# The first attention stage's score row: two transfers over DRAM in place of two TensorE transposes

## The chip, the cores and the metric

The kernel runs on one core of a Trainium2 chip. The metric is the device time of one execution in microseconds (us), as the median of several runs. A profile is one execution taken by the hardware profiler; its time is a little longer than that of a run without it. The engines are PE (TensorE matmul, with PEld for its weight loads), DVE (VectorE), ACT (ScalarE), POOL (GpSimd) and SP (SyncE, which here only issues DMAs).

## The reference: what is computed

64 graphs of 256 nodes with 256 features go through two layers. The first layer is two graph-attention stages, a layer norm, a feed-forward block and a layer norm; the second is attention over 8 heads with relations, and a feed-forward block. Only the first graph-attention stage matters here:

```python
def _gat(h, adj, W, a, out_features):
    Wh = jnp.matmul(h, W)
    Wh1 = jnp.matmul(Wh, a[:out_features])
    Wh2 = jnp.matmul(Wh, a[out_features:])
    e = Wh1 + jnp.swapaxes(Wh2, 1, 2)
    e = jax.nn.leaky_relu(e, negative_slope=ALPHA)
    scores = jnp.where(adj > 0, e, NEG)
    att = jax.nn.softmax(scores, axis=1)
    return jnp.matmul(att, Wh)
```

A score is the sum of one number of the one node (Wh1) and one number of the other (Wh2). With one of the nodes on the partitions, the numbers of those nodes are a column, one per partition, and the numbers of the others are a row of 256, which every partition needs in full. The change is about how that row gets to all partitions.

## The kernel before

All 64 graphs ("batches") are worked on at staggered stages. The work of a batch is cut into pieces with short names; the order in which all engines get them is written out by hand in three lists. PERIOD is one turn of the steady state: `F.fb/3` means that the piece F.fb is issued for the batch three behind the newest. It runs 58 times (batches enter it one by one, and the pieces of one turn belong to seven batches). START and END list the pieces of the first and the last batches with their batch numbers (`G.wh0:1` is batch 1, `T.out:-1` the last). Within an engine the instructions run in exactly this order; between engines, semaphores order them. All DMAs of the steady state go through SP's one queue, also in this order: an issue that waits for an engine holds up all later issues.

The pieces near the change, with their lines:

- G.wh0, G.wh1 (`project`, L847): PE multiplies the transposed input by the joint weights, which gives Wh and four columns of scores. G.wc0, G.wc1 (`keep`, L864): ACT copies the two halves to the SBUF tile wh_A. In PERIOD, wc0 of a batch is near the end of one turn and wc1 in the next.
- G.eA (`targets`, L870): two PE transposes of a score column of wh_A, each broadcast over 128 columns first, so that the row of 256 arrives in every partition of a PSUM tile e.
- G.lrA (`terms`, L884): ACT adds the other column as a bias and applies ReLU, from e in PSUM to s in SBUF, one instruction for each half of the nodes. G.adA (`maximum`, L893 to L899): DVE adds the row's linear part, masks, and takes the maximum. G.exA (`exps`, L910): ACT takes exponentials, from e to s. G.gA0, G.gA1 (`first`, L930): PE multiplies by Wh.
- G.eB to G.gB are the same for the second graph-attention stage; G.gB (`second`, L930, tile gat_b) is PE's last use of the buffer s in a batch. s has one buffer for both stages and all batches.
- The `turned` helper (L542, L546, L553) turns a tile by 32 x 32 squares on DVE (dt), writes it to DRAM (dm, tiles far_...) and reads it back as columns in four transfers (mg). It serves the attention's probabilities p (far_p, then pm, keys 10, 11, 01, 00) and the layer norms' outputs (far_y_a and cols_a after the first norm, far_y_y and cols_y after the second, far_y_c and cols_c after the third).
- F.qa to F.qe (L967, tile qX, qY, qZ): PE's projections to queries and keys, which read cols_y. F.sB (L676, tile S_y): POOL's sums of blocks of cols_y for the same projections.

PSUM has 8 banks for all products, given out in turn (`mm_tile`). DMAs share 8 semaphores in turn, so an issue also waits for the landing of the eighth before it.

The turn's order around the change, as it was (a piece of PERIOD): `F.nmB/3 T.hk1/5 G.lnA/2 T.hb/5 F.dtB/3 T.hk2/5 G.rsA/2 T.hp1/5 A.sp01/4 A.dm01/4 T.hc/5 A.mg10/4 T.hk3/5 G.nmA/2 F.raB/4 F.dtA/2 T.hd/5 A.vk2/4 G.most/1 T.hp3/5 G.eA/1 T.hp2/5 T.ge0/5 F.dmB/3 F.dmA/2`.

Of the kernel before, what the change touches and what calls it, by code (L numbers as in the profile page):

```python
# [25 lines left out]
F32 = mybir.dt.float32  # L26
# [8 lines left out]
P = 128  # L35
# [14 lines left out]
F.nmB/3 T.hk1/5 G.lnA/2 T.hb/5 F.dtB/3 T.hk2/5 G.rsA/2 T.hp1/5 A.sp01/4 A.dm01/4 T.hc/5 A.mg10/4  # L50
T.hk3/5 G.nmA/2 F.raB/4 F.dtA/2 T.hd/5 A.vk2/4 G.most/1 T.hp3/5 G.eA/1 T.hp2/5 T.ge0/5 F.dmB/3
F.dmA/2 T.fp2/6 A.sp00/4 A.vc/4 A.vp1/4 T.rbC/5 A.vk3/4 T.he/5 A.pm13/4 F.mgB/3 A.vp3/4 A.pm10/4
F.sB/3 G.lrA/1 F.mgA/2 A.vd/4 A.pm11/4 T.ge1/5 G.wh0/0 T.hk4/5 T.fe/6 G.wc0/0 F.qa/3 T.ge2/5
F.qk1/3 A.vp2/4 A.dt00/4 F.qb/3 A.ve/4 F.qk2/3 G.adA/1 F.qc/3 F.qk3/3 F.qp1/3 F.sA/2 F.ha/2 F.qp3/3
T.ge3/5 G.exA/1 F.qd/3 F.qp2/3 T.fk4/6 A.vk4/4 T.u0/5 F.hb/2 F.qe/3 A.mg01/4 F.hk1/2 A.sc1/3
T.lnD/6 F.hp1/2 A.mx11/3 F.hk2/2 A.dm00/4 A.pm03/4 A.mg00/4 T.u1/5 A.mx13/3 F.hc/2 A.mx10/3 F.hk3/2
A.ex13/3 A.mx12/3 T.rsD/6 L.adj/0 F.hp3/2 F.qk4/3 F.hd/2 A.pm02/4 F.hp2/2 A.ex12/3 A.pm01/4
# [10 lines left out]
G.wh0:0 G.wc0:0 G.wh1:0 G.wc1:0 G.eA:0 S.wf:0 S.f0:0 W.b:8 G.lrA:0 G.away:0 G.adA:0 G.exA:0 G.rzA:0  # L68
G.gA1:0 L.xT:2 G.most:0 L.adj:1 L.xT:1 S.f1:0 G.gA0:0 G.wd1:0 G.wd0:0 G.eB:0 G.wh0:1 G.lrB:0
G.adB:0 G.exB:0 W.b:3 S.wk:0 L.xT:3 G.rzB:0 G.wh1:1 W.c:8 S.wv:0 G.gB:0 G.lnA:0 S.f2:0 G.rsA:0  # L70
G.wc0:1 G.wc1:1 G.eA:1 S.v0:0 S.q0:0 G.lrA:1 S.p0:0 W.d:1 G.nmA:0 G.wh1:2 F.dtA:0 G.away:1 F.dmA:0
G.adA:1 G.exA:1 F.mgA:0 G.wh0:2 G.wh1:3 F.sA:0 G.rzA:1 F.ha:0 S.q1:0 F.hb:0 F.hk1:0 F.hk2:0 S.j1:0
S.lr:0 F.hc:0 F.hk3:0 F.hd:0 L.x:1 F.hp1:0 G.gA0:1 F.hp3:0 F.hp2:0 F.raA:0 F.rbA:0 F.r0:0 F.he:0
F.r1:0 G.gA1:1 F.hk4:0 F.r3:0 F.r2:0 G.most:1 F.u0:0 L.adj:2 G.wd1:1 F.u1:0 W.d:7 G.wd0:1 F.fa:0
F.fb:0 F.u3:0 G.eB:1 S.j2:0 F.fk1:0 S.lx:0 F.fk2:0 F.u2:0 F.fc:0 F.fk3:0 F.fd:0 G.lrB:1 G.adB:1
F.fp2:0 F.fp1:0 G.away:2 G.exB:1 F.fe:0 F.fp3:0 G.rzB:1 G.wc1:3 F.fk4:0 S.q2:0 F.lnB:0 G.wc1:2
F.rsB:0 G.gB:1 F.nmB:0 G.lnA:1 G.wc0:2 G.eA:2 F.dtB:0 G.rsA:1 G.nmA:1 G.most:2 F.raB:0 G.wh0:3
W.b:7 F.raA:1 F.dtA:1 F.dmB:0 F.mgB:0 F.dmA:1 G.lrA:2 W.a:3 W.b:4 G.adA:2 F.sB:0 F.qa:0 G.exA:2
F.qb:0 G.wc0:3 F.qk1:0 F.qk2:0 F.qc:0 F.rbA:1 F.qk3:0 G.rzA:2 F.qp3:0 F.mgA:1 F.qd:0 F.sA:1 F.qp2:0
A.sc1:0 L.xT:4 A.mx12:0 F.qe:0 A.mx10:0 L.adj:3 F.ha:1 G.away:3 A.ex12:0 F.hk1:1 F.qk4:0 A.mx11:0  # L80
F.hb:1 S.p2:0 F.hk2:1 F.hc:1 F.hk3:1 A.rz12:0 F.hp1:1 F.qp1:0 A.sp12:0 A.mx13:0 F.hd:1 A.ex10:0
F.hp2:1 A.sc0:0 L.x:3 A.ex13:0 A.rz13:0 A.sp13:0 A.ex11:0 F.hp3:1 A.mx00:0 A.rz11:0 F.he:1 F.r0:1
S.v1:0 G.gA1:2 F.hk4:1 A.mx03:0 S.lw:0 L.x:2 F.r1:1 A.rz10:0 A.sp11:0 G.gA0:2 A.mx02:0 S.v2:0
F.r3:1 F.r2:1 A.sp10:0 A.dt10:0 F.fa:1 G.wd1:2 F.u0:1 A.dt11:0 G.wd0:2 G.eB:2 A.dm10:0 G.lrB:2
F.fk1:1 F.fb:1 F.u1:1 A.mx01:0 F.fp1:1 F.fk2:1 F.u3:1 A.ex03:0 F.fc:1 F.fk3:1 A.ex02:0 F.u2:1
A.dm11:0 F.fd:1 G.adB:2 G.exB:2 F.fp2:1 L.x:4 F.fp3:1 A.rz03:0 A.mg10:0 S.v3:0 G.rzB:2 F.fe:1
G.most:3 F.fk4:1 F.lnB:1 F.rbB:0 A.mg11:0 F.rsB:1 A.rz02:0 G.gB:2 G.wh1:4 F.nmB:1 A.vb:0 A.va:0
A.sp02:0 G.lnA:2 F.dtB:1 A.vk2:0 A.ex00:0 G.rsA:2 G.nmA:2 A.ex01:0 A.vk1:0 S.l0:0 A.vc:0 F.dtA:2
F.dmB:1 F.raB:1 A.rz01:0 A.vp1:0 F.dmA:2 G.wh0:4 A.vk3:0 A.pm11:0 A.sp03:0 S.l1:0 A.rz00:0 F.mgB:1
G.eA:3 G.lrA:3 F.sB:1 A.vd:0 F.mgA:2 G.wc0:4 A.vp2:0 F.qa:1 A.sp01:0 A.sp00:0 F.qb:1 F.qk1:1  # L90
A.vp3:0 A.dt01:0 F.qk2:1 A.dm01:0 A.ve:0 G.wc1:4 F.qc:1 L.xT:5 F.sA:2 F.qp1:1 F.qk3:1 G.adA:3
F.ha:2 F.qd:1 F.hk1:2 A.vk4:0 F.qp3:1 A.dt00:0 A.mg01:0 G.exA:3 F.qp2:1 A.pm12:0 F.hb:2 F.hp1:2
A.sc1:1 F.hk2:2 G.rzA:3 F.hc:2 A.pm10:0 A.mx12:1 A.mx13:1 A.dm00:0 A.ex12:1 F.raA:2 A.pm13:0
A.mx11:1 A.o1:0 A.rz12:1 A.ex13:1 F.rbA:2 A.rz13:1 L.adj:4 F.hk3:2 A.mx10:1 G.gA0:3 F.hd:2 F.qe:1
A.ex10:1 A.mg00:0 A.sp13:1 G.wd0:3 A.ex11:1 A.sp12:1 F.hp3:2 G.gA1:3 A.rz10:1 F.qk4:1 G.wd1:3
A.pm02:0 F.hp2:2 A.sp10:1 A.rz11:1 A.pm03:0 A.sp11:1 F.r0:2 A.oc1:0 A.dt11:1 F.r1:2 F.he:2 A.pm00:0
A.dm11:1 F.hk4:2 F.r2:2 F.r3:2 A.pm01:0 G.eB:3 A.dt10:1 A.sc0:1 F.u0:2 A.mx03:1 G.lrB:3 A.o0:0
A.oc0:0 G.adB:3 A.dm10:1 A.ex03:1 F.u1:2 F.u3:2 F.fa:2 T.wo:0 F.fk1:2 F.u2:2 G.exB:3 F.fb:2 T.lnC:0
T.rsC:0 A.mg11:1 F.fk2:2 F.fc:2 S.l2:0 A.mx00:1 G.rzB:3 F.fk3:2 F.fd:2 F.fp1:2 T.nmC:0 A.vb:1
A.ex00:1 F.fp2:2 F.fe:2 A.mg10:1 T.dtC:0 F.fp3:2 A.mx02:1 G.gB:3 T.dmC:0 A.ex02:1 F.fk4:2 F.lnB:2  # L100
F.rsB:2 A.va:1 A.vk1:1 A.vk2:1 A.vc:1 F.nmB:2 T.mgC:0 A.rz03:1 G.wh0:5 A.mx01:1 G.eA:4 G.away:4
G.lnA:3 G.rsA:3 A.vk3:1 F.dtB:2 A.rz02:1 G.most:4 A.vd:1 A.rz00:1 G.wc0:5 F.dmB:2 G.nmA:3 A.sp03:1
T.sC:0 F.dtA:3 T.ha:0 G.lrA:4 T.hk1:0 A.vp2:1 T.hb:0 A.vp1:1 A.ex01:1 F.mgB:2 F.dmA:3 A.rz01:1
A.sp02:1 T.hk2:0 A.sp01:1 A.ve:1 T.hc:0 G.adA:4 A.dt01:1 A.sp00:1 A.vk4:1 T.hk3:0 F.sB:2 T.hd:0
T.hp2:0 F.qa:2 G.exA:4 T.raC:0 F.qk1:2 F.qb:2 F.qk2:2 F.qc:2 T.hp3:0 A.dt00:1 A.pm11:1 F.qk3:2
F.mgA:3 T.he:0 F.qd:2 T.ge0:0 F.sA:3 T.ge1:0 F.qp3:2 T.hp1:0 T.hk4:0 A.pm13:1 T.ge2:0 F.qp2:2
F.ha:3 A.dm01:1 T.ge3:0 F.qp1:2 F.hk1:3 A.vp3:1 F.hb:3 A.sc1:2 F.qe:2 F.hk2:3 F.rbB:1 A.mx10:2
F.qk4:2 A.dm00:1 T.rbC:0 F.hp1:3 A.mg01:1 A.mg00:1 A.mx12:2 A.pm12:1 A.mx11:2 F.hc:3 A.pm10:1
A.mx13:2 A.pm02:1 F.hk3:3 T.fa:0 A.pm03:1 T.u0:0 A.ex11:2 A.ex13:2 A.rz13:2 F.hd:3 A.ex12:2
A.ex10:2 G.rzA:4 A.pm00:1 F.hp2:3 T.fb:0 T.u1:0 A.sp13:2 A.pm01:1 T.fk1:0 A.rz11:2 A.o1:1 A.o0:1  # L110
A.rz10:2 F.raA:3 A.oc1:1 A.oc0:1 F.hp3:3 F.r1:3 L.adj:5 A.rz12:2 F.he:3 T.u3:0 F.hk4:3 F.r2:3
T.fp1:0 T.wo:1 A.sp12:2 T.fk2:0 A.dt11:2 T.lnC:1 T.fc:0 A.sp11:2 G.away:5 A.sp10:2 F.r3:3 A.dm11:2
T.fk3:0 T.fp3:0 T.rsC:1 F.rbA:3 G.gA1:4 F.r0:3 T.nmC:1 A.sc0:2 F.u0:3 A.mx02:2 F.fa:3 G.wd1:4
A.ex02:2 G.gA0:4 F.fk1:3 A.mx03:2 A.dt10:2 T.dtC:1 A.mg11:2 F.u1:3 A.rz02:2
# [4 lines left out]
T.u2:-6 F.fp1:-3 A.vk1:-4 T.dmC:-5 A.pm13:-4 G.rzB:-2 T.mgC:-5 F.fe:-3 A.ex01:-4 A.vb:-4 F.fk4:-3  # L119
T.sC:-5 G.gB:-2 F.lnB:-3 G.eA:-1 T.fd:-6 F.rsB:-3 A.sp02:-4 A.ex00:-4 A.vk2:-4 F.nmB:-3 A.vp1:-4  # L120
G.lnA:-2 A.vc:-4 G.lrA:-1 A.mg10:-4 T.fp2:-6 G.rsA:-2 T.ha:-5 F.dtB:-3 A.vk3:-4 A.rz03:-4 T.hk1:-5
A.rz00:-4 G.nmA:-2 A.rz01:-4 A.sp01:-4 L.x:-1 G.adA:-1 T.hp1:-5 T.hb:-5 A.sp03:-4 T.hk2:-5
# [88 lines left out]
def binary(ctx: ExitStack, tc: tile.TileContext, t, most, out: bass.AP):  # L211
# [612 lines left out]
    def gat(do, b, tiles):  # L824
# [40 lines left out]

        def targets(step, col):

            t["e"] = mm_tile(f"e_{step}{b}", (P, NT, N))
            for i in range(NT):
                nc.tensor.transpose(  # L870
                    parts(t["e"])[:, 0, 2 * i : 2 * i + 2],
                    t["wh", step][:, i, col : col + 1].to_broadcast([P, P]), ident,
                )
# [4 lines left out]
        def terms(step, col):  # L878
            if "early s" in tiles:
                s = t["s"] = tiles["early s"]  # L880
            else:
                s = t["s"] = work.tile([P, NT, N], F32, tag="s", name=f"s_{step}{b}", bufs=1)
            for j in range(NT):
                nc.scalar.activation(  # L884
                    parts(s)[:, j], parts(t["e"])[:, 0], AF.Relu,
                    bias=t["wh", step][:, j, col : col + 1],
                )

        def maximum(step):

            s, e = parts(t["s"]), parts(t["e"])
            for j in reversed(range(NT)):
                nc.vector.scalar_tensor_tensor(  # L893
                    e[:, j], e[:, 0], ALPHA / (1.0 - ALPHA), s[:, j], ALU.mult, ALU.add
                )
# [52 lines left out]
        for step, src, tgt, width in (("A", SRC1, TGT1, X2), ("B", SRC2, TGT2, D)):  # L948
            do[f"G.e{step}"] = partial(targets, step, tgt)
            do[f"G.lr{step}"] = partial(terms, step, src)  # L950
            do[f"G.ad{step}"], do[f"G.ex{step}"] = partial(maximum, step), partial(exps, step)
            do[f"G.rz{step}"] = partial(over_sums, step, width)
# [529 lines left out]
```

## Time and profile before

| | |
|---|---|
| median of 3 runs | 2992.03 us (2991.58 to 2992.23) |
| the profiled execution | 2993.21 us |
| span of its instructions | 2991.4 us |
| granted TensorE clock over the span | 0.995 |
| DMA queue of SP | 399,984 packets, 442.14 MB, 46.7% of 16 engines' time |
| matmul of e_A (L870) | x124 in the page's tile view and x4 in early batches, 273 ns each |
| ReLU of stage A (L884) | 457 ns each |

How to read the profile: the busy share of an engine counts the union of its instructions' times. Matmuls are pipelined and their ends are modelled, so what a matmul costs PE is read from the start of one to the start of the next. L12 is line 12 of the kernel before. In the timeline a row is: start in us from the span's start, duration in us, engine, line, operation, what it writes <- what it reads, and how many; in brackets, the idle time of the engine before it and what ended that. SP's rows are issues of DMAs: their duration is that of the issue, not of the transfer. In the chain of waits, a row is a start, a duration and what took it.

### The profile page before, as it was taken

To read this page: it belongs to the slowest core of one execution; us is meant where nothing else is said; L and a number is where in the kernel's file an instruction comes from. 1 tells how busy PE (TensorE), PEld (TensorE's weight loads), DVE (VectorE), ACT (ScalarE), POOL (GpSimd) and SP (SyncE) were. 2 spreads that over 40 slices of the span, in tenths; PEclk is the share of its full clock that TensorE was granted. 3 is DMA by queue.
4 is the path that set the end of the run, shared out by engine and by line. 5 is a ranking of instruction groups with operands and counts; after the bars stand their busy time and mean duration, and the time that the engine had idled before them with its cause. 6 is when DMAs were issued, how large, how long until landed. Compare 5 with 4: busy or idle time off the path is not lost.

```text
span 2991.4 us, 75422 instructions
## 1 busy us (share of the span) xinstructions
PE 2947.1 (99%) x25662; PEld 2672.7 (89%) x25662; DVE 2599.5 (87%) x6247; ACT 2232.7 (75%) x6404; POOL 2281.8 (76%) x3455
## 2 busy tenths in 40 slices
PE   8999999999999999999999999999999999999997
PEld 7889999989999999999899899999999998898985
DVE  4888888888889888888898898898888898888885
ACT  3677787787787777777777777777877877877764
POOL 6777777777777777777778778777777787777785
PEclk9999999999999999999999999999999999999999
DMA  5545445445445444444444454454454444444442
GB/s 140 156 149 160 149 150 155 155 146 159 150 152 158 148 149 155 149 152 155 151 155 153 153 156 150 152 159 145 150 161 150 149 158 150 147 158 148 135 156 86
DMA packets 401891, 449.27 MB, mean 150 GB/s; under 512 B 41152, under 2 KB 342720, under 8 KB 401504
## 3 DMA queue, kind: packets, MB, share of 16 engines
q1 hardware_dynamic: 399984, 442.14, 46.7%
q8 instruction: 209, 3.42, 0.5%
q0 software_dynamic: 976, 1.72, 0.3%
q14 instruction: 178, 1.46, 0.2%
q10 hardware_dynamic: 544, 0.52, 0.1%
HBM read 242.90 MB, written 201.33 MB: 148 GB/s over the span
## 4 chain that ended last, share of the span: by engine, by line
PE 90%; POOL 3%; DVE 2%; DMA 2%; issue 1%; SPq 1%; ACT 0%; POOLq 0%; DVEq 0%; ACTq 0%
PE hX_a L758 8%; PE o L1082 8%; PE fX_a L796 7%; PE fX_c L796 7%; PE hX_c L758 7%; PE sc L1024 5%; PE wo L1103 4%; PE hY_a L758 4%; PE qX L967 4%; PE fY_c L796 4%; PE hY_c L758 4%; PE fY_a L796 3%; PE gat_a L930 3%; PE gat_b L930 3%; PE wh L847 3%; PE vX L991 3%
## 5 line engine op out<-in xcount | busy, mean ns | idle before, releaser
L1071 DVE SCALAR_TENSOR_TENSOR pm<-away,pm 128x512 f32<-128x512 uint8 x512 | 356.8, 708 | 4.4 <-DMA pm<-far_p 4.0
L542 DVE STREAM_TRANSPOSE p<-p 128x1024 f32<-128x1024 f32 x256 | 315.4, 1232 | 4.1 <-POOL p L1057 4.1
L1082 PE MATMUL o<-pm,v 128*32 128x256 f32 x4096 | 235.9, 381 | 0.0
L776 ACT ACTIVATE hid_c<-hid_c,col_L_gnn_b 128x256 f32<-128x256 f32 x512 | 231.5, 505 | 1.8 <-DVE hid_c L734 0.4
L776 ACT ACTIVATE hid_a<-hid_a,col_L_gnn_b_ff 128x256 f32<-128x256 f32 x512 | 224.2, 501 | 2.4 <-DVE hid_a L734 2.2
L796 PE MATMUL fX_a<-f_L_gnn_w_ff,hid_a 128*128 128x128 f32 x1536 | 203.8, 276 | 1.7 <-DVE acc_a L734 1.3
L796 PEld LDWEIGHTS fX_a<-f_L_gnn_w_ff,hid_a 128*128 128x128 f32 x1536 | 196.0, 192 | 10.5 <-DVE acc_a L734 2.4
L796 PE MATMUL fX_c<-f_L_gnn_W,hid_c 128*128 128x128 f32 x1536 | 203.5, 275 | 0.8 <-DVE acc_c L734 0.4
L1082 PEld LDWEIGHTS o<-pm,v 128*32 128x32 f32 x4096 | 126.6, 110 | 85.7 <-DVE pm L1071 1.1
L796 PEld LDWEIGHTS fX_c<-f_L_gnn_W,hid_c 128*128 128x128 f32 x1536 | 191.8, 192 | 5.6 <-DVE acc_c L734 0.6
L676 POOL TENSOR_TENSOR S_y<-cols_y 128x128 f32<-128x128 f32 x128 | 66.3, 518 | 121.1 <-DMA cols_y<-far_y_y 120.8
L770 ACT COPY hid_a<-hX_a 128x512 f32<-128x512 f32 x192 | 113.1, 589 | 60.5 <-PE hX_a L758 60.2
L1024 PE MATMUL sc<-kT,qT 32*128 32x256 f32 x2048 | 146.7, 400 | 2.5 <-DVE kT L988 2.4
L864 ACT COPY wh_B<-gat_a 128x258 f32<-128x258 f32 x124 | 46.3, 374 | 133.5 <-PE gat_a L930 133.5
L758 PE MATMUL hX_a<-S_a,f_L_gnn_w_ff 128*128 128x128 f32 x1024 | 144.1, 284 | 0.0
L758 PEld LDWEIGHTS hX_c<-cols_c,f_L_gnn_W 128*128 128x128 f32 x1024 | 131.0, 191 | 13.1 <-DVE hid_c L734 3.1
L758 PEld LDWEIGHTS hX_a<-S_a,f_L_gnn_w_ff 128*128 128x128 f32 x1024 | 124.0, 191 | 19.7 <-issue 19.2
L758 PE MATMUL hY_c<-S_c,f_L_gnn_W 128*128 128x128 f32 x1024 | 139.5, 279 | 0.0
L758 PE MATMUL hX_c<-cols_c,f_L_gnn_W 128*128 128x128 f32 x1024 | 135.3, 275 | 2.9 <-DVE hid_c L734 2.5
L796 PE MATMUL fY_a<-f_L_gnn_w_ff,H_a 128*128 128x128 f32 x1024 | 137.3, 277 | 0.8 <-DVE acc_a L809 0.6
L796 PE MATMUL fY_c<-f_L_gnn_W,H_c 128*128 128x128 f32 x1024 | 136.0, 276 | 1.5 <-POOL H_c L676 0.9
L758 PE MATMUL hX_a<-cols_a,f_L_gnn_w_ff 128*128 128x128 f32 x1024 | 136.0, 276 | 0.4 <-DMA cols_a<-far_y_a 0.3
(2844 smaller groups left out, 10562.5 us busy)
## 6 DMA issues: line engine op xcount, KB each, us to landing
far_p<-p SPq DMA_DIRECT2D x256, 512.0 KB, 3.0
pm<-far_p SPq DMA_DIRECT2D x1024, 128.0 KB, 3.0
adj<-in_adjT SPq DMA_DIRECT2D x64, 256.0 KB, 3.4
far_y_a<-sq_a SPq DMA_DIRECT2D x64, 256.0 KB, 2.1
cols_a<-far_y_a SPq DMA_DIRECT2D x256, 64.0 KB, 2.0
far_y_y<-sq_y SPq DMA_DIRECT2D x64, 256.0 KB, 2.0
cols_y<-far_y_y SPq DMA_DIRECT2D x256, 64.0 KB, 2.0
far_y_c<-sq_c SPq DMA_DIRECT2D x64, 256.0 KB, 2.0
```

The costliest lines, as they stand in the source:

```text
L542: nc.vector.transpose(to, rows)
L758: nc.tensor.matmul(ps[:, f * P : (f + 1) * P], weights()[0][:, factor, f * P : (f + 1) * P], left, start=start and f == 0, stop=f == FC // ...
L770: nc.scalar.copy(hidden(i, h), ps.rearrange("p (f n) -> p f n", n=P))
L776: nc.scalar.activation(tiles["hid"][:, f, :], tiles["hid"][:, f, :], func, bias=b1[:, f : f + 1])
L796: nc.tensor.matmul(ps, left[:, f, :], weights()[2][:, factor, f * P : (f + 1) * P], start=start and f == 0, stop=f == FC // 2 - 1, skip_gr ...
L847: nc.tensor.matmul(t["whp", j], tiles["xT"][:, c, nodes(j)], wx[:, c, :], start=(c == 0), stop=(c == KC - 1),)
L930: nc.tensor.matmul(ps, t["s"][:, j, nodes(i)], t["whz"][:, j, :width], start=(j == 0), stop=(j == NT - 1),)
L967: nc.tensor.matmul(ps[:, nodes(n)], w[:, factor, :], right, start=start and n == 0, stop=n == 1, skip_group_check=True,)
L1024: nc.tensor.matmul(t["sc", g, hh][:, i, :], qkv["q"][hd, g, nodes(i)], qkv["k"][hd, g, :], start=True, stop=True,)
L1071: nc.vector.scalar_tensor_tensor(pm[:, 1], tiles["away"].rearrange("p (a n) -> p a n", a=4), 0.0, pm[:, 0], ALU.is_equal, ALU.mult,)
L1082: nc.tensor.matmul(ps[hh * DH : (hh + 1) * DH, :], qkv["v"][:, j, d0 : d0 + DH], t["pm", (g, hh)][:, r].rearrange("p a (j t r) -> p j t a ...
L1103: nc.tensor.matmul(t["wo"][:, i, :], t["oT"][:, c, nodes(i)], late["wo"][:, c, :], start=(c == 0), stop=(c == KC - 1),)
```

## The change

The targets' row of stage A no longer goes through PE. A new piece G.ewA writes the score column of wh_A (one number of each node, 256 runs of 4 bytes) to a DRAM tile of 256 numbers, and a new piece G.erA reads those 256 numbers back into all 128 partitions of the first half of s. Both are issued by SP. The ReLU of stage A then reads the row from s in SBUF and writes to e in PSUM, where it read from e and wrote to s; DVE's sum reads the row from s and the ReLU's result from e. Stage B stays as it was.

```diff
+        def leave(step, col):
+            t["far"] = far.tile([NT, P], F32, tag="farE", name=f"far_e_{step}{b}", bufs=8)
+            with nc.allow_non_contiguous_dma(reason="one number of a node"):
+                nc.sync.dma_start(
+                    out=t["far"].rearrange("t p -> p t"), in_=t["wh", step][:, :, col]
+                )
+
+        def back(step):
+            if "early s" in tiles:
+                t["s"] = tiles["early s"]
+            else:
+                t["s"] = work.tile([P, NT, N], F32, tag="s", name=f"s_{step}{b}", bufs=1)
+            nc.sync.dma_start(
+                out=t["s"][:, 0, :], in_=t["far"].rearrange("t p -> (t p)").partition_broadcast(P)
+            )
...
         def terms(step, col):
-            if "early s" in tiles:
-                s = t["s"] = tiles["early s"]
+            if step == "A":
+                t["e"] = mm_tile(f"e_{step}{b}", (P, NT, N))
+                to, row = parts(t["e"]), t["s"][:, 0, :].rearrange("p (a n) -> p a n", a=4)
             else:
-                s = t["s"] = work.tile([P, NT, N], F32, tag="s", name=f"s_{step}{b}", bufs=1)
+                if "early s" in tiles:
+                    t["s"] = tiles["early s"]
+                else:
+                    t["s"] = work.tile([P, NT, N], F32, tag="s", name=f"s_{step}{b}", bufs=1)
+                to, row = parts(t["s"]), parts(t["e"])[:, 0]
             for j in range(NT):
                 nc.scalar.activation(
-                    parts(s)[:, j], parts(t["e"])[:, 0], AF.Relu,
+                    to[:, j], row, AF.Relu,
                     bias=t["wh", step][:, j, col : col + 1],
                 )
...
             for j in reversed(range(NT)):
+                row, relu = e[:, 0], s[:, j]
+                if step == "A":
+                    row, relu = t["s"][:, 0, :].rearrange("p (a n) -> p a n", a=4), e[:, j]
                 nc.vector.scalar_tensor_tensor(
-                    e[:, j], e[:, 0], ALPHA / (1.0 - ALPHA), s[:, j], ALU.mult, ALU.add
+                    e[:, j], row, ALPHA / (1.0 - ALPHA), relu, ALU.mult, ALU.add
                 )
...
-            do[f"G.e{step}"] = partial(targets, step, tgt)
+            if step == "A":
+                do["G.ewA"], do["G.erA"] = partial(leave, step, tgt), partial(back, step)
+            else:
+                do["G.eB"] = partial(targets, step, tgt)
```

In the lists the two pieces are put in, and nothing else is moved. In PERIOD, G.ewA stands ahead of A.dm01 (the write of far_p, key 01) and G.erA where G.eA was, after A.mg10 (the four reads of pm, key 10) and ahead of F.dmB (far_y_y):

```diff
-F.nmB/3 T.hk1/5 G.lnA/2 T.hb/5 F.dtB/3 T.hk2/5 G.rsA/2 T.hp1/5 A.sp01/4 A.dm01/4 T.hc/5 A.mg10/4
-T.hk3/5 G.nmA/2 F.raB/4 F.dtA/2 T.hd/5 A.vk2/4 G.most/1 T.hp3/5 G.eA/1 T.hp2/5 T.ge0/5 F.dmB/3
+F.nmB/3 T.hk1/5 G.lnA/2 T.hb/5 F.dtB/3 T.hk2/5 G.ewA/1 G.rsA/2 T.hp1/5 A.sp01/4 A.dm01/4 T.hc/5
+A.mg10/4 T.hk3/5 G.nmA/2 F.raB/4 F.dtA/2 T.hd/5 A.vk2/4 G.most/1 T.hp3/5 G.erA/1 T.hp2/5 T.ge0/5
+F.dmB/3 F.dmA/2
```

In START, batches 0, 1 and 2 have the two pieces next to each other where G.eA was (for batch 2 right ahead of F.dtB:0, with F.dmB:0, that is far_y_y of batch 0, as the next issue); for batches 3 and 4, and in END for the last, G.ewA stands some pieces ahead of G.erA.

## The prediction

> **What bounds the kernel now.** I read the page first, then PE's timeline through one period, then SP's and ACT's over the same stretch, then who waited for whom.
>
> ```profile
> span 2991.4 us, 75422 instructions
> ...
> PE 2947.1 (99%) x25662; PEld 2672.7 (89%) x25662; DVE 2599.5 (87%) x6247; ACT 2232.7 (75%) x6404; POOL 2281.8 (76%) x3455
> ```
>
> PE is the bound, but a busy share with modelled ends proves little, so I took starts. From the first matmul of one gat_b to the next, 51 steady periods (the 10th to the 60th) give 45.11 to 45.19 us in 40 of them and up to 45.91 in 11. The floor of 45.11 is PE issuing without a pause.
>
> PE's timeline of one period (start, duration, what):
>
> ```profile
> 1506.12 1.06 PE L758 MATMUL hX_c<-S_c,f_L_gnn_W 128*128 128x128 f32 x8
> 1507.01 0.38 PE L870 MATMUL e_A<-ident,wh_A 128*128 128x128 f32 x2
> 1507.23 0.60 PE L991 MATMUL vX<-f_Wv,S_y 128*128 128x256 f32 x2
> ...
> 1510.30 1.05 PE L796 MATMUL fX_c<-f_L_gnn_W,hid_c 128*128 128x128 f32 x8
> 1511.19 0.39 PE L967 MATMUL qX<-cols_y,f_Wq 128*128 128x128 f32 x2
> ```
>
> The two transposes of e_A show 0.38 us, but the next product starts 0.22 us after them: matmuls overlap, and 0.22 us is what they hold PE for. qX, the first reader of cols_y, starts 11.80 us after this period's gat_b (at 1499.39).
>
> Who waited for whom (total us, times, longest):
>
> ```profile
> POOL S_y L676 <- DMA cols_y<-far_y_y: 120.8, 63, 4.2
> ...
> PE qX L967 <- DMA cols_y<-far_y_y: 5.2, 8, 1.8
> ```
>
> POOL waits for cols_y in nearly every period, PE in few. cols_y is thus the transfer with the least cover. In the 51 periods its fourth part lands 10.64 to 12.38 us after gat_b; where it lands after 11.66, qX starts 0.14 us behind the landing and the period is long. That happens in 10 of 51 and makes 10 of the 11 long periods; the mean stall over all 51 is 0.07 us.
>
> SP in the same period, and two rows of ACT:
>
> ```profile
> 1496.03 0.40 SPq L359 DMA_DIRECT2D xT<-in_xT  x1
> 1498.45 0.34 SPq L546 DMA_DIRECT2D far_p<-p  x1
> 1498.84 2.23 SPq L553 DMA_DIRECT2D pm<-far_p  x4
> 1503.85 0.34 SPq L546 DMA_DIRECT2D far_y_y<-sq_y  x1
> 1506.24 0.34 SPq L546 DMA_DIRECT2D far_y_a<-sq_a  x1
> 1506.67 2.52 SPq L553 DMA_DIRECT2D cols_y<-far_y_y  x4
> ```
>
> ```profile
> 1500.30 0.35 ACT L864 COPY wh_A<-wh 128x260 f32<-128x260 f32 x1
> ...
> 1508.75 0.82 ACT L884 ACTIVATE s_A<-e_A,wh_A 128x256 f32<-128x256 f32 x2
> ```
>
> SP works in order. It has 2.8 us free between pm and far_y_y, and cols_y follows far_y_a at once: far_y_y, landed 2.03 us (median) after its issue, was in by then. The slack of far_y_y's landing is 0.75 us.
>
> **Removed: PE.** Two transposes a batch at 0.11 us each, by start to start: 0.22 us x 64 = **14.0 us** gained if PE then still waits for nothing more.
>
> **Added and moved: SP.** In the changed kernel SP's order is xT, the column's write (G.ewA), far_p, four pm, the row's read (G.erA), far_y_y, far_y_a, four cols_y. The write waits for wh_A's copy, which ends at 1500.65. Step by step in this period:
>
> - Write: issued at 1500.68, 0.40 us (xT has as many runs, 256). So far_p is issued at 1501.12 in place of 1498.45, 2.67 us late, and pm ends at 1503.74.
> - Row's read: needs the write landed, at 1502.7 if it takes 2.0 us as the 256 KB writes do, at 1503.6 if it takes the 2.9 us of the one undisturbed load of 1024 four-byte words (the bias column col_L_gnn_b at 45.2 us). Either is hidden behind pm. It is issued at 1503.78, 0.43 us. The buffer s is free: gat_b ended by 1501.4.
> - far_y_y: issued at 1504.25, only 0.40 us late. But in before the queue was empty then; now it is not. In the trace the packets are served in the order of issue: far_p's 4096-byte packets end 2.56 us after its issue, pm's 512 packets of 1024 bytes follow and end 4.59 (10th percentile), 4.84 (median) or 5.39 (90th) after it. With 4.7, pm's data end at 1505.8. The row's 128 packets: between 0.37 (46 ns, 8 to an engine) and 0.57 us (a quarter of pm's time), taken 0.45. far_y_y's own packets take 0.82 us, and the landing comes 0.36 us behind the last: 1507.45, that is 8.06 us after gat_b in place of 6.49.
> - cols_y then starts at 8.11 in place of 7.29. The last part lands 3.81 us later on average (3.28 at least), and far_y_y's own scatter, 0.24 us on average, now counts in full.
> - PE without the transposes wants cols_y at 11.66 - 0.22 = 11.44. So the mean stall is 8.11 + 0.24 + 3.81 - 11.44 = 0.72 us a period, 0.65 more than now. The written period runs 58 times: **+37.7 us**.
>
> This landing is the cost that the trace does not show, so both ends: with no queue in front, far_y_y lands 2.03 after its issue, at 6.9, and the same sum over the 51 pairs of scatter gives a stall of 0.16 (+5.2 us over 58 periods); with pm's 90th percentile and 0.57 for the row it lands at 8.87, stall 1.53 (+84.7 us). I take 8.06, since the rows with a full queue stand nearest: in the period that I read packet by packet none overtook.
>
> **START.** For batch 2 the write and the read stand directly ahead of batch 0's far_y_y, and nothing else is between:
>
> ```profile
> 68.37 0.36 ACT L864 COPY wide<-wh 128x260 f32<-128x260 f32 x1
> ```
>
> ```profile
> 68.79 2.02 DMA far_y_y<-sq_y
> ```
>
> The second line is from the chain that ended last. The read waits until the write has landed (68.76 + 2.0) and takes 0.43, so far_y_y goes out at 71.25: **+2.5 us**, at least 0 if later work absorbs it. In batch 0 the two transfers delay the ReLU by some 3.8 us, and gat_a, at 22.24, has 4.3 us to spare after whz_A (17.95): nothing. Batch 1's gat_a (50.76) comes 7.5 us after its whz_A: nothing.
>
> **Costed at nothing.** The ReLU now reads SBUF and writes PSUM: 457 ns today from PSUM to SBUF; n_d, from SBUF to PSUM, takes 582 where its SBUF twin y_b takes 594, so between -0.01 and +0.13 us each, taken +0.04; ACT idles 0.27 us before the second qT, which hides it. If that were gone, qT and kT would be late for DVE. The ReLU waits for the row at 1507.1 (pm's landings come 0.82 us behind their last packet) and runs at 1508.75, so 1.6 us hide it; without them the GELU pieces and wh_A's copy behind it on ACT are late, and fX_c after them. DVE has one operand in PSUM and one in SBUF, as before. The bank e is taken at the ReLU instead of at the transpose, with no other bank taken between. far_p and pm late by 2.7 us: pm landed at 1503.86 and DVE masks this buffer at 1509.69, p's buffer is refilled at 1520.81.
>
> **A rule against it.** No write to DRAM in before has runs under 1 KB; the new one has 256 runs of 4 bytes, and the nearest rows are the bias columns, whose 64-byte packets take 25 ns (median). The Trainium skill, DMA: Bandwidth & Descriptors, Specifications, says that below 512 bytes the engines read, modify and write. No row here shows what that costs on a write; if it held the queue for a further 0.5 us, every period would pay nearly all of it, 29 us more than my sum.
>
> **The rivals.**
> 1. Forecast, 0.55: the queue carries the delay into cols_y. 2993.2 - 14.0 + 37.7 + 2.5 = **3019.4 us** (2998 to 3040).
> 2. Faster, 0.13: far_y_y passes the queue nearly unhindered and lands by 7.0; the stall stays at 0.16, and the start absorbs its part: 2993.2 - 14.0 + 5.2 = 2984.4. For it: SP itself is only 0.40 us late, and 0.75 is to spare. Against it: packets in order of issue. It decides at a landing of 7.4, where the stall eats the 14 us.
> 3. Nothing measurable, 0.12: a landing at 7.1 to 7.5 us: 2986 to 2998.
> 4. Worse, 0.20: the four-byte runs cost SP or the queue 0.5 us or more (the bias column of 1024 words takes 0.94 us to issue on POOL): landing at 8.5 to 9, 3045 to 3075, and the row's read may then wait for the write too.
>
> **The numbers.** The sum stands on the profiled execution (2993.21; its span 2991.4), 1.2 us above the median of 2992.03. I predict 3019. The range, 2985 to 3060, reaches from rival 2's time to within rival 4's, and leaves out some 0.07 below and 0.08 above. A difference under 0.2% (6 us) can't be told from none here: faster 0.13, same 0.12, slower 0.75.
>
> **What would show it.** In the changed profile: vX 0.11 to 0.12 us after hX_c, with no e_A on PE; the column's write starting at the end of wh_A's copy and far_p right behind it, 1.7 us after gat_b's start; far_y_y landing near 8.06 us; PE's waits led by qX <- cols_y with some 42 us in place of 5.2. Wrong if far_y_y lands by 7.2, if ACT waits for the row, or if PE's new wait is not at qX.

## The result and the profile after

The changed kernel takes **3634.28 us** (median of 4 runs, 3628.97 to 3636.65) where the kernel before took 2991.81 beside it (4 runs, 2990.44 to 2992.23): a ratio of 1.2146, 95% interval 1.2125 to 1.2167. I had said 3019, with 2985 to 3060 as the range: slower was right, but by some 640 us in place of 27, and far beyond the range. The profiled execution has a span of 3627.2 us, 635.8 more than before.

The page of the changed kernel: PE's busy time has grown by 139 us although it does less, and the share has dropped from 99% to 85%.

```profile
span 3627.2 us, 75478 instructions
...
PE 3085.8 (85%) x25534; PEld 2786.3 (77%) x25534; DVE 2611.5 (72%) x6247; ACT 2250.9 (62%) x6404; POOL 2269.0 (63%) x3455
```

Who waited for whom in the changed kernel (total us, times, longest):

```profile
POOL S_y L677 <- DMA cols_y<-far_y_y: 624.2, 62, 13.5
...
PE qX L995 <- DMA cols_y<-far_y_y: 459.7, 62, 13.3
ACT e_A L906 <- DMA s_A<-far_e_A: 372.9, 60, 14.3
DVE pm L1099 <- DMA pm<-far_p: 249.3, 59, 5.5
```

The new wait is where I had put it, at qX, but 11 times as large as my 42 us; and pm and the row, which I had called covered, are waited for too (ACT's wait for the row was one of my signs of being wrong). SP's rows of a steady period (gat_b starts at 1835.44; start, duration of the issue, what):

```profile
1836.74 0.38 SPq L870 DMA_DIRECT2D far_e_A<-wh_A  x1
1837.24 0.39 SPq L547 DMA_DIRECT2D far_p<-p  x1
1837.67 2.40 SPq L554 DMA_DIRECT2D pm<-far_p  x4
1847.00 0.34 SPq L879 DMA_DIRECT2D s_A<-far_e_A  x1
1847.44 0.38 SPq L547 DMA_DIRECT2D far_y_y<-sq_y  x1
1847.87 0.42 SPq L547 DMA_DIRECT2D far_y_a<-sq_a  x1
1851.61 1.74 SPq L554 DMA_DIRECT2D cols_y<-far_y_y  x4
```

The column's write is issued 1.30 us after gat_b, far_p 1.80 and pm 2.23 after it: as forecast. The row's read, which needs the write landed, goes out 11.56 us after gat_b (median 11.10) where I had 4.39. far_y_y stands behind it, and cols_y starts at 16.17 (median 16.36) in place of 8.11. The chain of waits of the changed kernel has the write itself on it; these are three of its 25 longest pieces (start, duration, what), the first of them in batch 2:

```profile
91.28 9.74 DMA far_e_A<-wide
233.50 10.45 DMA far_e_A<-wh_A
564.38 9.84 DMA far_e_A<-wh_A
```

So a write of 1 KB takes some 10 us to land. And it doesn't do so alone. Stretches of the changed kernel (length, busy us of each engine with its instructions, granted clock, busy share of the DMA engines, GB/s): far_p's transfer, then the stretch up to the row's read, then pm's rest and the row. The busy times stand in the order PE, PEld, DVE, ACT, POOL.

```profile
1836.70:1839.10 2.40, 2.40 (x20) 2.32 (x20) 1.81 (x6) 1.43 (x5) 2.15 (x6) 1.00 0.47 166
1839.10:1847.00 7.90, 7.90 (x60) 7.28 (x59) 6.19 (x13) 4.70 (x9) 5.76 (x10) 1.00 1.32 32
1847.00:1849.50 2.50, 0.37 (x4) 0.18 (x2) 0.42 (x1) 0.00 (x0) 0.00 (x0) 1.00 0.86 199
```

The same view of the kernel before, while pm is read:

```profile
1501.00:1503.50 2.50, 2.50 (x22) 2.42 (x21) 2.08 (x6) 1.60 (x4) 2.25 (x7) 1.00 0.75 195
```

For 8 us the DMA engines are shown busier than ever (1.32) and move 32 GB/s in place of some 195. That pair, a high share with next to no bytes, is how the hold-up shows in this profile. The packets tell the same: the 256 four-byte packets are over 2.4 us after gat_b, in 0.2 us, but of pm's 1024-byte packets, issued behind them, the last starts 13.37 us after gat_b (median of 51 periods; 3.84 in before).

PE in the same period:

```profile
1843.07 0.60 PE L1019 MATMUL vX<-f_Wv,S_y 128*128 128x256 f32 x2
1843.51 0.59 PE L1019 MATMUL vY<-f_Wv,S_y 128*128 128x256 f32 x2
1844.01 1.16 PE L759 MATMUL hX_c<-cols_c,f_L_gnn_W 128*128 128x128 f32 x8
...
1846.32 1.05 PE L797 MATMUL fX_c<-f_L_gnn_W,hid_c 128*128 128x128 f32 x8
1855.12 0.77 PE L995 MATMUL qX<-cols_y,f_Wq 128*128 128x128 f32 x2 [7.74 <-DMA cols_y<-far_y_y]
1855.68 0.63 PE L995 MATMUL qX<-cols_y,f_Wk 128*128 128x128 f32 x2
1856.11 0.63 PE L995 MATMUL qZ<-cols_y,f_Wq 128*128 128x128 f32 x2
```

The pause at qX is 7.74 us, and it has a second price: the pairs of products behind it start 0.42 us apart where the same pairs start 0.22 apart in before. The stretches with PE's columns alone (length, busy, granted clock, DMA) show why:

```profile
1847.00:1851.00 4.00, 0.37 (x4) 1.00 0.84 224
...
1855.00:1857.00 2.00, 1.88 (x9) 0.50 0.53 158
1857.00:1859.00 2.00, 2.00 (x9) 0.50 0.98 272
1859.00:1861.00 2.00, 2.00 (x19) 0.96 0.47 190
```

After the pause TensorE is granted half its clock for some 4 us. In medians, qX starts 8.0 us later than in before, and hX_a, the first product after the block of projections, 9.75 later: **1.7 us of the loss in each period is slow clock**, not waiting.

Where the 635.8 us lie, by the starts of gat_b: the tenth comes 93.7 us late; the next 51 periods take 55.22 us in place of 45.21 on average (510.2); what follows costs 31.9.

### The profile page after: what moved, and what is told of

Same layout as the page of the kernel before. It is cut to its first block, busy times and chain, and to the rows that moved or that the text cites. A ratio compares the mean times of both kernels' runs of the same rounds, so it can differ in the third digit from the quotient of the medians.

```text
span 3627.2 us, 75478 instructions
## 1 busy us (share of the span) xinstructions
PE 3085.8 (85%) x25534; PEld 2786.3 (77%) x25534; DVE 2611.5 (72%) x6247; ACT 2250.9 (62%) x6404; POOL 2269.0 (63%) x3455
## 4 chain that ended last, share of the span: by engine, by line
PE 58%; DMA 23%; DVE 10%; SPq 3%; issue 3%; POOL 2%; ACT 1%; another core or an unknown queue 0%; POOLq 0%; DVEq 0%; ACTq 0%
DMA far_e_A<-wh_A 10%; DMA far_y_y<-sq_y 8%; PE hX_a L759 7%; PE o L1110 6%; PE qX L995 5%; PE sc L1052 4%; DMA cols_y<-far_y_y 3%; PE wo L1131 3%; PE fX_c L797 3%; PE hY_a L759 3%; PE fY_c L797 3%; PE gat_a L955 3%; PE fX_a L797 3%; SPq L554 3%; PE qY L995 2%
## 5 line engine op out<-in xcount | busy, mean ns | idle before, releaser
L995 PE MATMUL qX<-cols_y,f_Wq 128*128 128x128 f32 x256 | 72.5, 373 | 459.7 <-DMA cols_y<-far_y_y 459.7
L677 POOL TENSOR_TENSOR S_y<-cols_y 128x128 f32<-128x128 f32 x128 | 58.5, 457 | 624.2 <-DMA cols_y<-far_y_y 624.2
L995 PEld LDWEIGHTS qX<-cols_y,f_Wq 128*128 128x128 f32 x256 | 50.4, 246 | 471.5 <-issue 469.4
L906 ACT ACTIVATE e_A<-s_A,wh_A 128x256 f32<-128x256 f32 x122 | 58.2, 477 | 374.9 <-DMA s_A<-far_e_A 372.9
L1012 ACT ACTIVATE qT<-qX,col_L_gnn_bq 128x128 f32<-128x128 f32 x192 | 70.4, 367 | 175.3 <-PE qX L995 175.3
L677 POOL TENSOR_TENSOR H_c<-hid_c 128x512 f32<-128x512 f32 x64 | 81.1, 1267 | 133.7 <-ACT hid_c L777 133.7
L759 PE MATMUL hX_c<-cols_c,f_L_gnn_W 128*128 128x128 f32 x1024 | 143.2, 283 | 19.4 <-DMA cols_c<-far_y_c 12.0
```

The lines of the kernel that those rows point to most:

```text
L677: engine.tensor_tensor(to[i], one, other, op)
L759: nc.tensor.matmul(ps[:, f * P : (f + 1) * P], weights()[0][:, factor, f * P : (f + 1) * P], left, start=start and f == 0, stop=f == FC // ...
L995: nc.tensor.matmul(ps[:, nodes(n)], w[:, factor, :], right, start=start and n == 0, stop=n == 1, skip_group_check=True,)
```

## The experiments

Theories. **T1**: the write holds up the DMAs behind it, because its words are small or lie together in DRAM. **T2**: my forecast, SP's wait for wh_A's copy and the order behind it. **T3**: the row's read is what stalls. **T4**: four-byte runs are slow wherever they go. Runs 1 to 4 and later 5 to 8 stood beside one another on a chip, with the kernel before at 2996.6 and 2994.2 us. A time without a number of runs or an interval is one execution; those of the kernel before lay between 2990 and 2998 us throughout, so a few us between two such times say nothing. Beside each time stand three medians over the same 51 periods: mean period, start of cols_y's issues and start of qX after gat_b (before: 45.21, 7.29, 11.80; after the change: 55.22, 16.36, 19.82).

### The write alone, the read alone (e1, e2)

```diff
...
-                do["G.ewA"], do["G.erA"] = partial(leave, step, tgt), partial(back, step)
+                do["G.ewA"], do["G.erA"] = partial(leave, step, tgt), partial(targets, step, tgt)
```

> The column's write stays at its place, nobody reads it; the row comes from the two PE transposes again, the ReLU as before the change. T1 (the write of 256 four-byte runs to DRAM lands about 9 us after its issue and holds up all transfers behind it): far_y_y and cols_y stay late, 3450 to 3640 us. T2 (my forecast: only the wait for wh_A's copy shifts far_p, pm and far_y_y): 3015 to 3040. T3 (the row's read is what stalls): 2995 to 3040.

Measured: **3617.18 us** (55.22, 16.26, 19.75).

For e2, `leave` does nothing and `back` does the transposes and `nc.sync.dma_start(out=t["s"][:, 0, :], in_=x[b, 0].partition_broadcast(P))`.

> No column write; at the read's place SP issues a broadcast of one 1 KB row of the input x from DRAM to the first half of s in 128 partitions; the row of scores comes from PE's transposes, and the ReLU overwrites what the broadcast brought. T1: the read is harmless, 2992 to 3010 us. T3 (128 reads of one KB of DRAM stall the queue): 3400 or more. T2: 2993 to 3005, since the wait for wh_A's copy is gone.

Measured: **2995.80 us** (45.23, 7.27, 11.80). T3 has fallen: a broadcast with no write ahead of it costs nothing. In e1 the write, which nobody reads, brings the steady period of the whole change to the hundredth. The profiled spans of e1 and of the whole change differ by 11.9 us; 9.0 of them are there by the tenth gat_b, in the start, where the change waits for the row itself (first gat_b at 43.6 us in the change, 37.3 in e1, 30.8 before). The waits of e1:

```profile
POOL S_y L677 <- DMA cols_y<-far_y_y: 627.8, 62, 12.2
...
PE qX L979 <- DMA cols_y<-far_y_y: 449.7, 61, 9.7
```

### The same words to SBUF; longer runs to DRAM (e3, e4)

```diff
...
-                nc.sync.dma_start(
-                    out=t["far"].rearrange("t p -> p t"), in_=t["wh", step][:, :, col]
-                )
+                nc.sync.dma_start(out=t["s"][:, :, 0], in_=t["wh", step][:, :, col])
```

> As the run with the write alone, but its 256 four-byte runs go to the first column of s in SBUF (which waits for gat_b's end too, some 0.7 us later than wh_A's copy, and which the ReLU then overwrites). T1 with DRAM as the cause: 3005 to 3060 us. T4 (four-byte runs are slow whatever they are written to): 3400 or more. T2: 3030 to 3060.

Measured: **3097.76 us** (46.82, 9.25, 13.32): 38 us above my bound, but 519 below the same words to DRAM. The write waits for gat_b here and goes out 1.97 us after its start, so far_p goes at 2.67, 0.9 later than in e1; that is part of the excess, the rest is open.

```diff
-            t["far"] = far.tile([NT, P], F32, tag="farE", name=f"far_e_{step}{b}", bufs=8)
+            t["far"] = far.tile([NT, P, P], F32, tag="farE", name=f"far_e_{step}{b}", bufs=8)
...
-                    out=t["far"].rearrange("t p -> p t"), in_=t["wh", step][:, :, col]
+                    out=t["far"].rearrange("t p n -> p t n"), in_=t["wh", step][:, :, :P]
```

> As the run with the write alone, but the runs are 512 bytes in place of 4 (the first 128 numbers of each node of wh_A, 256 runs, 128 KB, to a DRAM tile that nobody reads). T1 with the size of the run as the cause: the write costs about 1 us of the queue, 3015 to 3070 us. T4' (256 runs to DRAM from this place are slow whatever their size): 3400 or more. T2: 3020 to 3060.

Measured: **3035.46 us** (45.71, 8.21, 12.14). As many runs, 128 times the bytes, no hold-up. T4 and the number of runs are out as the main cause: it takes short runs, and either DRAM as such or their lying side by side there. e3 doesn't part these two, since in s no two of its words are neighbours; neighbouring words in SBUF were not tried.

### How the words lie in DRAM (e5 to e8, e18)

All are the write alone. e5: `out=t["far"][:1]...`, `in_=t["wh", step][:, :1, col]`. e6, e7 and e18 write one word into each of 256 places of a tile `[NT, P, n]` with n = 16, 128 and 4; e8 fills `[NT, P, 16]` with `in_=t["wh", step][:, :, :16]`.

e5, 128 words:

> As the run with the write alone, but with 128 four-byte runs (the first half of the nodes) in place of 256. If each word costs its own time one after another (some 9 us for 256, so about 35 ns each), the hold-up shrinks by about 4 us a period: 3340 to 3430 us. If it is a fixed cost of such a write: 3600. T2: 3020 to 3040 in any case, which the write alone already spoke against.

e6, words 64 bytes apart:

> As the run with the write alone, but the 256 words lie 64 bytes apart in DRAM (over 16 KB) in place of next to each other. If words that share a block of DRAM are what is slow (one after another into the same place): 3020 to 3100 us. If every four-byte write to DRAM is slow wherever it goes: 3550 to 3650.

e7, words 512 bytes apart:

> The same with the words 512 bytes apart (over 128 KB, the layout of the 512-byte runs, of which 4 bytes are written). Shared blocks as the cause: 3020 to 3060 us, no slower than the words 64 bytes apart, and faster if a block is larger than 64 bytes. Shortness alone as the cause: 3550 to 3650.

e8, runs of 64 bytes:

> The same with runs of 64 bytes, next to each other (the first 16 numbers of each node, 16 KB). If what counts is whether a block of 64 bytes is written in full: 3015 to 3050 us. If blocks of 512 bytes or more are written one part after another: slower than the words 512 bytes apart, 3200 or more.

e18, words 16 bytes apart:

> The write alone with its 256 words 16 bytes apart (4 to a block of 64 bytes, over 4 KB). If the hold-up goes by the words that share a block, one after another (about 0.55 us for each further one, from cols_y's start of 16.26 us with 16 and 8.19 with 1): cols_y starts near 9.8 us, 3100 to 3150 us. If it goes by the number of words in blocks that are not written alone: as with neighbouring words, 3500 to 3620.

In the last column, the median start of pm's last packet less that of far_p's last one, in us (before: 2.5, the changed kernel: 9.3), which shows the hold-up itself:

| | us | period, cols_y, qX | pm's last packet |
|---|---|---|---|
| e1: 256 words, neighbours | 3617.18 | 55.22, 16.26, 19.75 | 10.8 |
| e5: 128 words, neighbours | 3271.97 | 49.25, 11.43, 14.96 | 8.6 |
| e18: 256 words 16 bytes apart | 3084.82 | 46.66, 9.41, 13.02 | 3.5 |
| e6: 256 words 64 bytes apart | 3030.68 | 45.72, 8.19, 12.22 | 2.8 |
| e7: 256 words 512 bytes apart | 3033.31 | 45.85, 8.22, 12.27 | 2.8 |
| e8: 256 runs of 64 bytes | 3026.08 | 45.67, 8.15, 12.04 | 2.8 |

The same 256 words in the same 0.2 us of packets: 64 bytes apart they hold pm up no longer than the 1 KB runs of e9 or the 512-byte runs of e4 do (2.7 to 2.8 in all three), as neighbours they hold it for 8 us more. 64 bytes apart, the write itself lands 1.6 us after its issue (median). The waits with the words 64 bytes apart, against 627.8 with neighbours:

```profile
POOL S_y L677 <- DMA cols_y<-far_y_y: 174.9, 63, 4.3
```

So **words that lie next to each other in DRAM** are the cause. The number of words alone doesn't decide: 128 neighbours still hold pm for 6.1 us (8.6 less the 2.5 of before), while 256 lone words hold nothing. It goes by how closely they lie: 16 to a stretch of 64 bytes 8.0 us (10.8 less the 2.8 of lone words), 4 to one 0.7, 1 to one nothing. That is steeper than in proportion (with my 0.55 us for each further word I had 3100 to 3150 for e18, and it took 3085), so a law isn't to be had from three points. If any two words in one block are enough, the block is no larger than 64 bytes; a larger block that bears a few words and not many isn't excluded (a stretch of 512 bytes gets 8 words in e6, 32 in e18, 128 in e1). Where I say "share a block" below, this is what is meant. e5 came out below its range since its write waits only for wh_A's first half and is issued 2.9 us ahead of gat_b, so that far_p goes out where it did in before; its time says less than its packets.

### The wait alone, and another queue (e9, e10)

e9: `far.tile([1, N], ...)` and `in_=t["wh", step][:1, 1, :N]`. e10: `nc.scalar.dma_start` for `nc.sync.dma_start`.

> The write alone again, at its place, but as one run of 1 KB out of one partition of wh_A (behind the same copy) to a DRAM tile that nobody reads; the row comes from PE's transposes. This leaves of the change only SP's wait for wh_A's copy and the place in the order. My forecast's term for it is a stall of about 0.5 to 0.7 us a period: 3015 to 3035 us. If the wait is covered and the 1.1 us that the 256 packets hold the queue are what counts: 2990 to 3005.

Measured: **3011.32 us** (before beside it 2994.86; 45.46, 7.98, 11.81): T2's wait and order by themselves cost 16 us, a little below the range. 256 separate runs in the same place (e4, e6 to e8, 3026 to 3035 us) cost another 15 to 24.

> The write alone, 256 neighbouring four-byte runs as in the change, but issued by ACT on a queue of its own, so that SP's order and waits are as before the change. If only the transfers behind it in the same queue are held up: 2995 to 3030 us. If the hold-up reaches the transfers of SP's queue all the same: 3300 or more.

Measured: **3527.48 us** (53.66, 7.51, 18.11). The write goes out on ACT's own queue, and SP is undisturbed up to cols_y, whose reads are then issued and transferred slowly:

```profile
1629.29 0.34 SPq L547 DMA_DIRECT2D far_y_y<-sq_y  x1
1631.67 0.34 SPq L547 DMA_DIRECT2D far_y_a<-sq_a  x1
1632.40 7.62 SPq L554 DMA_DIRECT2D cols_y<-far_y_y  x4
```

The hold-up isn't one of order within a queue. Part of this delay is SP waiting for the write's own landing, because the semaphores are shared in turn (185.4 us of SP's waits name far_e_A); but its first read was issued by then and takes 9.56 us to land (median; 2.16 in before), and its 512-byte packets crawl: from 9.8 to 16 us after gat_b, 6 start in 0.2 us, where the run with 512-byte writes (e4) has 29 (medians of 51 periods). Whether the DMA engines or DRAM behind them hold the data, the trace doesn't tell.

### Another place, another form (e11, e12)

Batches 5 to 62 have no transposes; the others keep them. In PERIOD, G.ewA stands behind A.mg10 and G.erA behind F.dmB. e12 adds the piece G.etA ahead of G.lnA and writes rows in place of words:

```diff
+            nc.vector.transpose(
+                t["s"][:, 1, :64].rearrange("p (t n) -> p t n", t=NT),
+                t["wh", step][:, :, col - 31 : col + 1],
+            )
...
+            t["far"] = far.tile([NT, 4, 32], F32, tag="farE", name=f"far_e_{step}{b}", bufs=8)
...
+                out=t["far"].rearrange("t k r -> k t r"),
+                in_=t["s"][31:P:32, 1, :64].rearrange("k (t r) -> k t r", t=NT),
```

> The whole change (no transposes for batches 5 to 62, the others keep them) with the write's words as in it, but with the write issued behind pm's four reads, where SP was idle, and the row's read behind far_y_y. If order is the cause (my forecast): 2978 to 3000 us. T1 (neighbouring words): far_y_y, the row's read and cols_y still stand behind the write: 3350 or more.

Measured: **3438.25 us** (52.84, 13.22, 17.38). Issued behind pm's reads, the words hold up far_y_y, the row's read and cols_y instead; the wait ahead of far_p isn't the cause.

> The same places as the run with the words later, but DVE first turns 32 columns of wh_A by squares, so that the row is written as 8 runs of 128 bytes. T1: no block of 64 bytes is shared, nothing is held up; 58 batches without their 0.22 us of transposes give up to 12.8 us: 2978 to 2995 us. If the write's mere landing time of two DMAs or the row's packets ahead of far_y_a and cols_y count: 2995 to 3015.

Measured: **2999.09 us** (11 runs) against 2994.86 (15 runs): 1.0014, interval 1.0005 to 1.0023 (45.34, 7.38, 11.77). 8 runs of 128 bytes hold up nothing (cols_y 7.38 for 7.29), and the transposes are gone; yet nothing is gained, and the time lies in the second range. The 14 us of my first term aren't there.

### Where the transposes' gain went (e13 to e16)

e13 reads `rows["L0_gnn_g_ln1"]` as the row, has no G.ewA and G.erA, and keeps G.eA for batches 0 to 4 and 63 alone. e14 is e13 with one piece moved, as shown here; e15 (the true row) and e16 (the kernel before) have the same move:

```diff
-A.vk3/4 T.he/5 A.pm13/4 F.mgB/3 A.vp3/4 A.pm10/4 F.sB/3 G.lrA/1 F.mgA/2 A.vd/4 A.pm11/4 T.ge1/5 G.wh0/0
+A.vk3/4 G.wh0/0 T.he/5 A.pm13/4 F.mgB/3 A.vp3/4 A.pm10/4 F.sB/3 G.lrA/1 F.mgA/2 A.vd/4 A.pm11/4 T.ge1/5
```

> Neither transposes nor transfers: in batches 5 to 62 the ReLU and DVE's sum read a row of a norm's weights that lies in SBUF anyway, in place of the row of scores (the scores of these batches are left out). My forecast's term: 58 x 0.22 = 12.8 us less than before, 2978 to 2983. If the transposes stand in the shadow of PE's wait for DVE's sum of hX_c (0.04 to 0.14 us a period is left): 2985 to 2993.

Measured: **2993.34 us** against 2994.58: 0.9996, interval 0.9986 to 1.0005 (45.22, 7.29, 11.77): no gain that can be told from none, and 0.3 us above the second range. PE's rows of this run, without any transposes:

```profile
1508.10 1.06 PE L758 MATMUL hX_c<-S_c,f_L_gnn_W 128*128 128x128 f32 x8
1508.99 0.60 PE L1008 MATMUL vX<-f_Wv,S_y 128*128 128x256 f32 x2
1509.43 0.59 PE L1008 MATMUL vY<-f_Wv,S_y 128*128 128x256 f32 x2
1509.94 1.16 PE L758 MATMUL hX_c<-cols_c,f_L_gnn_W 128*128 128x128 f32 x8
1510.93 0.60 PE L1008 MATMUL vX<-f_Wv,S_y 128*128 128x256 f32 x2
```

and the DVE row that stands between the two products hX_c:

```profile
1509.19 0.69 DVE L734 TENSOR_TENSOR hid_c<-hid_c,hX_c 128x512 f32<-128x512 f32 x1
```

The second hX_c goes into the same PSUM tile as the first, so it must wait until DVE has added the first one up: first product's end 1509.16, sum 1509.19 to 1509.88, second product 1509.94. PE has vX and vY to do meanwhile (0.87 us), and with the transposes (0.22 more) it was just busy enough not to notice. Starts after gat_b in undisturbed periods, before and e13: vX 7.85 and 7.63, hX_c 8.71 and 8.57, the next vX 9.60 and 9.57. Of 0.22 us, 0.04 are left (the second hX_c, which had to wait, takes longer too: 1.16 for 1.05).

> The same, with the product wh of the newest batch issued ahead of the product hX_c that waits for DVE, in place of behind the vX that follows it. If that wait is what hid the gain, it comes out now: 2978 to 2985 us. If something else sets the period: as without the move, 2985 to 2993.

Measured: **2987.38 us**, 0.9974 of before, interval 0.9963 to 0.9984 (45.09, 7.29, 11.59). That is 2 us above the range for this cause; what speaks for it is the 6.0 us to e13, from which only the move differs, and the rows. With wh as work in the meantime, PE runs through:

```profile
1503.79 0.60 PE L1008 MATMUL vX<-f_Wv,S_y 128*128 128x256 f32 x2
1504.23 0.60 PE L1008 MATMUL vY<-f_Wv,S_y 128*128 128x256 f32 x2
1504.66 1.04 PE L848 MATMUL wh<-wx,xT 128*128 128x260 f32 x4
1505.54 1.05 PE L758 MATMUL hX_c<-cols_c,f_L_gnn_W 128*128 128x128 f32 x8
```

The undisturbed period falls from 45.11 to 44.92 us; some of it is given back at cols_y, which now has 0.2 us less cover.

> The true row again, by DVE's squares and 8 runs of 128 bytes, with the squares put into the buffer of whz (which does not wait for gat_b, so DVE turns them while it is idle anyway), and wh ahead of hX_c. If both explanations hold: 58 x up to 0.22 gained, less some 2 to 6 us, since cols_y has 0.2 us less cover: 2982 to 2991. If the transfers cost more than the shadow: 2993 or more.

Measured: **2990.90 us**, 0.9988, interval 0.9979 to 0.9997 (45.20, 7.27, 11.59): the true row by squares, 128-byte runs and the move together are a little faster than the kernel before.

> The kernel before with only wh moved ahead of hX_c. With the transposes in place PE does not wait at hX_c, so there is nothing to gain: within 3 us of before, whatever the explanation; if it is faster by 5 us or more, the move is worth something by itself and e14 and e15 must be read against it.

Measured: **2996.64 us**, 1.0009, interval 1.0000 to 1.0018 (45.27, 7.29, 11.80). The move by itself gains nothing; it only lets the transposes' time come out.

### My own case (e17)

`far.tile([NT, P, 16], ...)`, `in_=t["wh", step][:, :, :16]`, and the row is read from `t["far"][0, :16]`.

> The changed kernel with its order, its waits, its row's read and no transposes, but the write takes 16 numbers of each node (256 runs of 64 bytes, 16 KB) in place of one, and the row that comes back is the first 1 KB of them, so the scores are left out. My forecast as it stands: 3019 us. With its term for the transposes (14.0) replaced by what the run without a row showed (about 1 to 2 us): 3028 to 3036. If the row's read costs more than the 0.45 us of queue: 3040 or more.

Measured: **3071.97 us** against 2996.32: 1.0257, interval 1.0237 to 1.0278 (46.23, 8.96, 12.67). With the hold-up taken out, the change as it stands still costs 76 us, not 27. By gat_b: the fourth is 15.0 us late, the 51 periods take 1.01 us more each. So of the span's 635.8 us, 79.6 are order, waits and read, and the difference, **some 556, goes with the shared blocks**. What the steady periods lose shows in far_y_y's time from issue to landing (last number), in the same line of three pages: before, e6 (write alone, no row's read) and e17:

```profile
far_y_y<-sq_y SPq DMA_DIRECT2D x64, 256.0 KB, 2.0
...
far_y_y<-sq_y SPq DMA_DIRECT2D x64, 256.0 KB, 3.5
...
far_y_y<-sq_y SPq DMA_DIRECT2D x64, 256.0 KB, 3.8
```

## Why the prediction was wrong, step by step

- **What bounds the kernel, and which transfer has the least cover: right.** PE's waits are led by qX <- cols_y in each run that was held up, and the period follows cols_y's start.
- **SP's order: right.** The write starts at the end of wh_A's copy, far_p 1.77 us after gat_b (1.73 forecast). By itself it costs 16 us (e9), and with the row's read and the start 76 (e17), so that slower was right for a reason of the forecast too.
- **The write's landing in 2.0 to 2.9 us: the step that failed.** I took the time from 256 KB writes with long runs and from a load of 1024 four-byte words, and treated the two bounds as enclosing a write of neighbouring words, of which the trace had no row at all. It lands in some 10 us, so that the row's read isn't hidden behind pm, and it takes the rest of the DMA traffic with it: 556 us of the 636. For the same words 64 bytes apart the bounds would have been safe: they land in 1.6 us (e6). The rival that came nearest was the fourth (four-byte runs cost 0.5 us or more): it named the right operation, but not what was wrong with it, for four-byte runs in places of their own cost no more than long ones. Its price of 29 us was a figure chosen by me and came from no row.
- **The rule against it**, that of the Trainium skill, DMA: Bandwidth & Descriptors, Specifications, on engines that read, modify and write below 512 bytes, spoke against the right operation. The runs show no price for a short run by itself: runs of 64 bytes (3026 us) and lone words 64 bytes apart (3031) cost no more than runs of 512 (3035). What hurt were words that share a block; whether by reading, modifying and writing it, no run here shows.
- **"Removed: PE, 14.0 us": wrong.** 0.22 us from start to start is what the transposes hold PE for, and vX did come 0.22 earlier; the condition that I had added, that PE then waits for nothing more, didn't hold one product further on. Without the transposes 58 batches gained 1.2 us (e13, an interval that includes none).
- **far_y_y through a full queue: too low.** In my own case cols_y starts at 8.96 us, not 8.11, with the row's read in front of far_y_y; without that read it is at 8.15 to 8.22. far_y_y lands at 8.94 us (median) where I had 8.06, past even my upper end of 8.87. Without the read it lands at 8.17 (e6), where my sum without its 0.45 gives 7.61. So both terms were too small, the read's by 0.3 us and the rest of the queue's by 0.6, and the mean period grows by 1.01 us, not by 0.43.
- **START, +2.5 us: wrong.** In my own case the fourth gat_b is 15.0 us late, in the changed kernel 36.8. For batches 0 and 1 I had looked at the ReLU's spare time alone. In e17 SP stands from 12.7 to 17.4 us waiting for the first write to land, and loads of weights and of xT that it issued from 6.9 to 15.3 us in before go out from 17.8 to 21.9, behind it; how much of the 15.0 us this makes, no run shows.
- **Costed at nothing.** The ReLU takes 477 ns in place of 457: right, and free. "1.6 us hide the row's wait" was wrong with the landing, but ACT's 372.9 us lie beside PE's wait: e1, where nobody reads the row, has the same period.
- **No step of mine** had the clock, which adds 1.7 us to each pause of 8.

## What to carry to other kernels

When a DMA writes single numbers, look at where neighbours land, not only at how many runs there are: neighbouring four-byte writes to DRAM held up every transfer here for 8 us, words 64 bytes apart or runs of 64 and 128 bytes didn't, and squares turned on an engine are a way to such runs. An operation that is removed from the bounding engine gains its time only as far as nothing later on that engine was waiting in its shadow; read the starts on to the first product that shares a buffer with another engine. Where the trace has no row for an operation, bounds from other operations don't enclose it, and the range has to say so.

## What the runs showed of the hardware

- 256 four-byte writes into 1 KB of DRAM landed in 8.8 to 10.5 us (the time from the write's issue to the row's read that waits for it, 51 periods), and for some 8 us of it the core's DMA moved 32 GB/s in place of 195; 64 bytes apart, the same writes landed in 1.6 us (median) and held up nothing. The hold-up reached the transfers of another queue (e10, 3527 us).
- After a pause of 7.7 us TensorE was granted 0.50 of its clock for some 4 us, and the starts of pairs of products that are 0.22 us apart in before were 0.42 apart. The Trainium skill, TensorE: Matmul & The Clock Gate, Part 1, has the same half rate after an idle window of some 3.4 us, until the array has been busy for about as long; its price of under 1% of a typical kernel is for the ramp alone, and the same part has a kernel that pays at every DMA wait. So it is here: the pause comes back in every period, and 1.7 us of 55 are 3%.
